# Holding result scatters back around the last norm, and giving each later product its own slot for one

## The chip, the cores and the metric

The kernel runs on one core of a Trainium2 chip. The time is device microseconds from start to end of one execution; of the kernel before there are six runs, median 702.27 us (700.46 to 706.06). Five engines work side by side, each with its own instruction queue in order: PE (TensorE, matrix products, with PEld for loading weights), DVE (VectorE), ACT (ScalarE), POOL (GpSimd) and SP (SyncE, which here only issues DMAs). They wait for each other through semaphores. DMAs move data between DRAM and the on-chip memory; indirect ones (scatter and gather by an index per row) are issued by POOL.

## The reference

The input x has 8 sequences of 512 tokens of width 128, in float32. Three residual blocks follow one another:

```
x = x + 0.5 * ffn(layernorm(x))
x = x + attention(layernorm(x))          # 16 heads of 8, causal, decay on half of the heads
x = x + 0.5 * ffn(layernorm(x))
```

The `ffn` is a mixture of 8 experts (128 -> 512 -> 128, relu) of which each token uses two: the router takes the two largest of eight logits and weighs the two results with a softmax over them:

```
logits = x @ router_w + router_b
topk_scores, topk_idx = top_k(logits, 2);  gates = softmax(topk_scores)
out = sum_e gate_e * (relu(x @ W1[e] + b1[e]) @ W2[e] + b2[e])
```

The reference computes all experts for all tokens; the kernel computes only the two that count.

## The kernel before

**Groups and rooms.** The tokens of the eight sequences are sorted to experts in groups: f0, f1, f2 for the first ffn, g0, g1, g2 for the second. Each expert has a room of fixed size in a DRAM buffer of the group (`xs`); for g1 and g2 it has 512 rows, in four tiles of 128. A group is filled by *token scatters* (`scatter` in `route`, L895): one indirect DMA for 128 tokens and one of their two experts, so 8 for a sequence. When all of a group's token scatters have landed, `experts` (L948 on) loads the rooms one expert at a time (`fetch`, L957), transposes them (`turn`, L1000, copied to `xT` at L1004), multiplies by W1 (`wide`, four products of 512 columns, L1013, relu at L1020) and by W2 (`out`, four tiles, L1037, bias added on DVE at L1041). Each of these is one *piece*; g1 and g2 have 72 pieces each, nine for a middle expert: four of the first product, four of the second product of the expert before, one of transposes.

**Results.** In g1 and g2 (the "tagged" groups) each row carries the number of its token's place. Each of the 32 tiles of results is sent back to that place in a second DRAM buffer (`ys`) by a *result scatter* (`send`, L981), an indirect DMA too. `out` only appends it to the list `results`. Later `collect` reads `ys` back in plain order (`yr`, L1140), multiplies by the gates, adds to x (L1144, L1148, L1154) and writes the output (L1157). The result tiles `ysb` have five buffers, one for each expert in flight.

**Order.** The order is written out by hand. The main part is a row of *units*: 96 units (0 to 95) are attention steps, units from 96 to 125 have no attention any more. `surround(n, att)` writes one unit: the attention step if there is one, a quota of pieces of the group that is being computed, the steps that are due in that unit (`due`: norm, router, projection, read-back, each a generator that is advanced by one step), and up to three *transfers*. `plan` says which group is opened in which unit (`close_group` and the first two `fetch`es), and between which units its pieces are spread: g1 from unit 79 to 106, g2 opened in unit 106 and spread from 107 to 125.

**Transfers.** `transfer` takes one indirect DMA from a list: token scatters and gathers (`jobs`) come first, results (`results`) when there are none. It is called at fixed places of a unit: after the first piece, in the middle (only from unit 96 on, when more than two wait), and at the end. POOL's queue takes them in the order in which they are written. `behind_mark` (L640 on) makes every one wait for the latest evacuation of a product that was written before it (`mark`), so a transfer can't start long before the place where it was written.

**The last sequence.** Sequence 7's attention is finished in unit 98. Its second norm and router (`route`) run three steps a unit: the norm in unit 99 (the reciprocal root of the variance, `rstd`, is a POOL instruction, L479, DVE's `xn` at L774 waits for it), transposes (L789), logits (L825) and ranks in unit 100, places (L869 to L885) in unit 101, where its eight token scatters join the list. They are the last of g2. Before, units 98 to 100 send eight results and unit 101 one before the first token scatter; the eight follow in units 101 to 103, each behind another piece; then results again, three a unit.

**The end.** After unit 125 the rest of the results is sent, then g2's read-back runs.

Of the kernel before, what the change touches and what calls it, by code (L numbers as in the profile page):

```python
# [49 lines left out]
CAP = max(cap for _, cap, _ in ROOMS)  # L50
NOWHERE = 1e6
CT = -(-CAP // P)
STOP = object()

def common_constants(nc, const, aps, names):
# [393 lines left out]
class Group:  # L449
# [3 lines left out]
    def __init__(self, shares, cap, key, xs, ys, tagged):  # L453
        self.shares, self.cap, self.key, self.xs, self.ys = shares, cap, key, xs, ys
        self.base, self.tiles = [], 0
        for _, t0, t1 in shares:
            self.base.append(self.tiles)
            self.tiles += t1 - t0
        self.tagged, self.width = tagged, D + 2 * tagged
        self.ct = -(-cap // P)  # L460
        self.rows = cap // self.ct
        assert self.ct * self.rows == cap
        self.parts = [(t, min(3 if cap > 4 * P else 4, self.ct - t))
                      for t in range(0, self.ct, 3 if cap > 4 * P else 4)]
        self.placed = 0
        self.pieces = E * (len(self.parts) * (1 + C) + self.ct) + 1


# [19 lines left out]
class Main:  # L488
    def __init__(self, tc, ctx, aps):
# [15 lines left out]


        self.jobs, self.results, self.mark = deque(), deque(), None
        self.adds, self.unit = deque(), 0
        const = self.const

# [144 lines left out]
    def transfer(self, second=False):  # L655

        if self.jobs and (
            not second or any(urgent for urgent, _ in self.jobs)
            or (len(self.jobs) > 4 and not self.results)
        ):  # L660
            self.jobs.popleft()[1]()
        elif self.results:
            self.results.popleft()()

    def additions(self):
# [282 lines left out]
    def experts(self, g):  # L948
# [31 lines left out]
        def send(e, t, ys):  # L980
            ins = nc.gpsimd.indirect_dma_start(  # L981
                out=g.ys[:, :],
                out_offset=bass.IndirectOffsetOnAxis(ap=home[e][:rows, t : t + 1], axis=0),
                in_=ys[:rows, t, :], in_offset=None,
            ).ins
            tc.declare_no_dep(ins, group=f"ys_{key}", reason="no two rows have the same home")
            tc.add_to_no_dep_group(f"ys_{key}", ins)
            self.in_turn(ins, scatter=True)
            self.behind_mark(ins)

        def up(e, xb):

# [3 lines left out]
            def turn(t0, nt):  # L996
                n0, n = t0 * rows, nt * rows
                tp = self.bank([P, N], f"xbT_ps_{key}_{e}_{t0}")
                for t in range(nt):
                    nc.tensor.transpose(  # L1000
                        tp[:, ts(t, rows)], xb[:rows, t0 + t, :D], self.ident[:rows, :rows]
                    )
                if self.evac == "act":
                    nc.scalar.copy(xT[:, n0 : n0 + n], tp[:, :n])  # L1004
                else:
                    nc.vector.tensor_copy(xT[:, n0 : n0 + n], tp[:, :n])
                if g.tagged and t0 == 0:
                    homes(e, xb)

            def wide(t0, nt, c):  # L1010
# [10 lines left out]
                else:  # L1021
                    ins = nc.vector.tensor_scalar(dst, z[:, :n], bias, 0.0, ALU.add, ALU.max)  # L1022
                self.mark = ins.ins

            return (
                h, [partial(turn, *p) for p in g.parts],
# [3 lines left out]
        def down(e, h):  # L1030
# [3 lines left out]
            def out(t):  # L1034
# [7 lines left out]
                    ys[:rows, t, :], y[:rows], self.b2_sb[:rows, e], ALU.add  # L1042
                )
                self.mark = ins.ins
                if g.tagged:
                    self.results.append(partial(send, e, t, ys))
                elif t == g.ct - 1:
                    nc.sync.dma_start(
                        g.ys[: E * g.cap, :].rearrange("(t p e) d -> e p t d", p=rows, e=E)[e],
                        ys[:rows, : g.ct],  # L1050
                    )
# [75 lines left out]
    def collect(self, g, i, dst, parts=1):  # L1127
# [5 lines left out]
        if i % 2 == 0:  # L1133
            self.pair = self.p2.tile([P, 2, T, 2, D], FP, tag="ee", name=f"yr_{b}")
        yr = self.pair[:, i % 2]
        src = g.ys[: 2 * P * g.tiles, :].rearrange("(t p r) d -> p t r d", p=P, r=2)
        n = -(-(end - first) // parts)
        for t in range(first, end, n):
# [202 lines left out]
def macaron_kernel(  # L1341
# [51 lines left out]
    with ExitStack() as main:  # L1393
# [61 lines left out]
        def combined(u, g, i, dst=None, urgent=False, ahead=False):  # L1455
# [2 lines left out]

        plan = [
            (f0, first, first, -16), (f1, -17, -16, 7), (f2, 5, 7, 43), (g0, 41, 43, 79),  # L1460
            (g1, 78, 79, tail - 1), (g2, tail - 2, tail - 1, ends),
        ]
        fills = {}

        def surround(n, att):

# [24 lines left out]
            m.evac = "dve" if att and n % seq not in (8, 9, 10) else "act"  # L1491
            if att:
                m.causal(units[n][2], ee, 0)
            run(take(fill, 1 if quota else 0))
            m.evac = "act"
            m.transfer()
            if last is not None:
                m.outputs(*last)
            if att:
# [5 lines left out]
            for k, (stream, steps) in enumerate(work):  # L1505
                some = todo // (len(work) - k + 1)
                run(take(stream, steps))
                run(take(fill, some))
                todo -= some
            if n >= core and len(m.jobs) + len(m.results) > 2:  # L1510
                run(take(fill, todo // 2))
                todo -= todo // 2
                m.transfer(second=True)
            run(take(fill, todo))
            m.additions()
            m.transfer(second=True)

        m.held = m.oT = None
        with m.banks(("m", 8)):
# [35 lines left out]
            for i in range(2):  # L1555
                combined(79 + 7 * i, g0, i, out)
            for i, (_, t0, t1) in enumerate(g1.shares):
                at(tail + 2 + 3 * i, m.collect(g1, i, out), 1 + t1 - t0)
            at(tail, m.verdict(bad), 2)

            for u in range(first, 0):
# [74 lines left out]
```

## Time and profile before

| | us |
|---|---|
| median of six runs | 702.27 (700.46 to 706.06) |
| profiled execution | 704.29 |
| its span, first to last instruction | 702.6 |
| PE busy in the span | 625.2 (89%) |
| POOL busy in the span | 295.6 (42%) |
| last product result evacuated on DVE | 683.2 |
| last result scatter landed | 688.06 |

The profile shows one execution. A line of its timeline gives the start and the length in us, the engine, the line of the kernel, the operation, what it writes `<-` what it reads, and in brackets how long the engine had stood idle and what ended that. A line of the waits gives who waited for whom, the total in us, how often, and the longest. A line of the stretches gives the stretch, its length, and for each engine the time it was busy in it with the number of instructions, then the clock granted to TensorE as a share of full speed, the share of time in which the DMA engines were busy, and GB/s. POOL counts an indirect DMA as busy for the time in which it issues it (about 0.97 us). TensorE's ends are modelled, not measured.

### The profile page before, as it was taken

To read this page: it belongs to the slowest core of one execution; us is meant where nothing else is said; L and a number is where in the kernel's file an instruction comes from. 1 tells how busy PE (TensorE), PEld (TensorE's weight loads), DVE (VectorE), ACT (ScalarE), POOL (GpSimd) and SP (SyncE) were. 2 spreads that over 40 slices of the span, in tenths; PEclk is the share of its full clock that TensorE was granted. 3 is DMA by queue.
4 is the path that set the end of the run, shared out by engine and by line. 5 is a ranking of instruction groups with operands and counts; after the bars stand their busy time and mean duration, and the time that the engine had idled before them with its cause. 6 is when DMAs were issued, how large, how long until landed. Compare 5 with 4: busy or idle time off the path is not lost. (4 is left out here: it accounts for less than half of the span.)

```text
span 702.6 us, 12913 instructions
## 1 busy us (share of the span) xinstructions
PE 625.2 (89%) x4797; PEld 406.0 (58%) x4797; DVE 411.5 (59%) x1426; ACT 347.7 (49%) x564; POOL 295.6 (42%) x318
## 2 busy tenths in 40 slices
PE   3269989999999999999989999999999988869980
PEld 2148857755656565556656656555565656647760
DVE  6736437745466575685677687778665644232433
ACT  4034333455565656556566565656746532234422
POOL 3744626654041214414143524332244455654550
PEclk9999999999999999999999999999999998979995
DMA  8746833221508961011201111112112021144225
GB/s 256 199 134 188 224 106 97 70 63 56 119 27 141 186 201 34 27 27 45 68 28 43 42 39 36 32 32 81 49 32 62 28 61 39 58 125 138 73 70 156
DMA packets 80230, 61.33 MB, mean 87 GB/s; under 512 B 7400, under 2 KB 73888, under 8 KB 80160
## 3 DMA queue, kind: packets, MB, share of 16 engines
q1 hardware_dynamic: 71296, 42.79, 23.8%
q0 software_dynamic: 8576, 17.63, 8.2%
q8 instruction: 40, 0.66, 0.4%
q14 instruction: 30, 0.25, 0.1%
q10 hardware_dynamic: 288, 0.01, 0.0%
HBM read 26.21 MB, written 34.19 MB: 86 GB/s over the span
## 5 line engine op out<-in xcount | busy, mean ns | idle before, releaser
L1245 ACT ACTIVATE ee<-st 128x768 f32<-128x768 f32 (+1 forms) x192 | 158.9, 880 | 93.2 <-PE st L1238 80.7
L1252 DVE TENSOR_TENSOR ee<-ee,keep 128x256 f32<-128x256 f32 (+1 forms) x192 | 97.9, 511 | 98.0 <-ACT ee L1245 92.7
L479 POOL DMA_INDIRECT yt_f<-ys,back_f x64 | 65.2, 1019 | 130.0 <-ACT h_f L1020 49.5
L1037 PEld LDWEIGHTS y_f<-w_sb,h_f 128*120 128x120 f32 (+1 forms) x704 | 85.9, 182 | 28.3 <-issue 15.8
L1238 PE MATMUL st<-qT,kT 32*128 32x512 f32 (+3 forms) x1024 | 96.1, 467 | 5.2 <-ACT ee L1245 3.2
L895 POOL DMA_INDIRECT xs<-xn_g,to_g x64 | 64.0, 1000 | 86.0 <-DVE x L1098 13.5
L1037 PEld LDWEIGHTS y_g<-w_sb,h_g 128*128 128x128 f32 x640 | 81.8, 194 | 31.1 <-issue 24.4
L1013 PE MATMUL z_g<-xT_g,w_sb 128*128 128x512 f32 (+1 forms) x192 | 90.3, 557 | 6.3 <-ACT xT_g L1004 6.3
L1037 PE MATMUL y_f<-w_sb,h_f 128*120 128x128 f32 (+1 forms) x704 | 94.0, 277 | 0.2 <-DVE h_f L1022 0.2
L1013 PE MATMUL z_f<-xT_f,w_sb 128*128 128x480 f32 (+1 forms) x192 | 91.3, 566 | 1.0 <-ACT xT_f L1004 1.0
L1264 PE MATMUL o<-ee,vpad 128*32 128x512 f32 (+3 forms) x1024 | 90.1, 444 | 1.1 <-DVE ee L1252 1.0
L1020 ACT ACTIVATE h_f<-z_f,b1T 128x480 f32<-128x480 f32 (+1 forms) x86 | 53.4, 622 | 68.0 <-PE z_f L1013 45.5
L1037 PE MATMUL y_g<-w_sb,h_g 128*128 128x128 f32 x640 | 86.5, 280 | 0.2 <-DVE h_g L1022 0.2
L981 POOL DMA_INDIRECT ys<-ysb_g,home_g x64 | 62.8, 981 | 51.1 <-ACT h_g L1020 20.4
L1020 ACT ACTIVATE h_g<-z_g,b1T 128x512 f32<-128x512 f32 (+1 forms) x77 | 49.3, 642 | 52.7 <-PE z_g L1013 42.6
L1238 PEld LDWEIGHTS st<-qT,kT 32*128 32x128 f32 x1024 | 43.1, 183 | 38.0 <-issue 15.4
L1041 DVE TENSOR_TENSOR ysb_g<-y_g,b_sb 128x128 f32<-128x128 f32 x80 | 23.0, 290 | 70.9 <-PE y_g L1037 47.5
L895 POOL DMA_INDIRECT xs<-xn_n,to_f x40 | 39.1, 977 | 37.9 <-issue 8.8
L1264 PEld LDWEIGHTS o<-ee,vpad 128*32 128x32 f32 x1024 | 23.9, 109 | 53.1 <-issue 15.1
L1041 DVE TENSOR_TENSOR ysb_f<-y_f,b_sb 120x128 f32<-120x128 f32 (+1 forms) x88 | 25.1, 289 | 49.8 <-PE y_f L1037 38.0
L1013 PEld LDWEIGHTS z_g<-xT_g,w_sb 128*128 128x128 f32 x192 | 30.4, 196 | 26.0 <-issue 15.5
L1013 PEld LDWEIGHTS z_f<-xT_f,w_sb 128*128 128x128 f32 x192 | 31.4, 200 | 15.4 <-issue 11.0
(187 smaller groups left out, 773.2 us busy)
## 6 DMA issues: line engine op xcount, KB each, us to landing
xs<-zeros SPq DMA_DIRECT2D x8, 520.0 KB
xb_g<-xs SPq DMA_DIRECT2D x16, 260.0 KB
w_sb<-in_L_ffn_W_dram SPq DMA_DIRECT2D x16, 256.0 KB
xb_f<-xs SPq DMA_DIRECT2D x16, 240.0 KB
ys<-ysb_f SPq DMA_DIRECT2D x16, 240.0 KB
ys<-zeros SPq DMA_DIRECT2D x2, 1664.0 KB
x<-in_L_attn_x_dram SPq DMA_DIRECT2D x8, 256.0 KB
xs<-zeros SPq DMA_DIRECT2D x1, 1920.0 KB
```

Of the source, the lines that this page charges most:

```text
L479: ins = op(*args, **kw)
L895: ins = nc.gpsimd.indirect_dma_start(out=g.xs[:, :], out_offset=bass.IndirectOffsetOnAxis(ap=to[:, t, r : r + 1], axis=0), in_=xn[:, t, : ...
L981: ins = nc.gpsimd.indirect_dma_start(out=g.ys[:, :], out_offset=bass.IndirectOffsetOnAxis(ap=home[e][:rows, t : t + 1], axis=0), in_=ys[:r ...
L1013: nc.tensor.matmul(z[:, :n], self.w1_sb[:, e, ts(c, P)], xT[:, n0 : n0 + n], start=True, stop=True,)
L1020: ins = nc.scalar.activation(dst, z[:, :n], AF.Relu, bias=bias)
L1037: nc.tensor.matmul(y[:rows], h[:, c, ts(t, rows)], self.w2_sb[:, e, c, :], start=(c == 0), stop=(c == C - 1),)
L1041: ins = nc.vector.tensor_tensor(ys[:rows, t, :], y[:rows], self.b2_sb[:rows, e], ALU.add)
L1238: nc.tensor.matmul(st[:, h, c0 : c0 + N - kt * P], kT[r0 : r0 + SLOT, ts(kt, P)], qT[r0 : r0 + SLOT, kt * P :], start=True, stop=True,)
L1245: nc.scalar.activation(ee[:, two, :width], st[:, two, :width], AF.Exp)
L1252: ins = self.nc.vector.tensor_tensor(d, d, self.keep.unsqueeze(1).unsqueeze(1).to_broadcast([P, 2, len(parts), P]), ALU.min,)
L1264: self.nc.tensor.matmul(self.o[h * SLOT : (h + 1) * SLOT, kt * P :], self.vpads[b % 2][:, kt, 4 * g + h, :], ee[:, h, c0 : c0 + n], start= ...
```

## The change

It has five parts, all behind or near the end of the 96 attention units.

1. `HOLD`: in units 97, 98 and 99 no result is sent (token scatters still are).
2. From unit 100 on the fixed places for transfers are gone. The token scatters that are in the list after a step are written at once, all in a row.
3. From unit 100 on a new wrapper, `pieces`, may send one result after each piece: when the counter `work` is at least `SPACING` (830), it calls `transfer` and takes 830 off. `work` counts the columns (or for transposes and results the like) of every piece written.
4. g2 is opened (count, and the first two loads) in unit 105, not 106. Its pieces still begin in unit 107.
5. g1's four read-backs begin in units 113, 116, 119 and 122, not 110, 113, 116 and 119. An assertion says that all results of the group have been sent by then.

```diff
--- before.py
+++ after.py
@@ -50,6 +50,8 @@
 CAP = max(cap for _, cap, _ in ROOMS)
 NOWHERE = 1e6
 CT = -(-CAP // P)
+SPACING = 830
+HOLD = (97, 98, 99)
 STOP = object()
 
 def common_constants(nc, const, aps, names):
@@ -462,7 +464,7 @@
         assert self.ct * self.rows == cap
         self.parts = [(t, min(3 if cap > 4 * P else 4, self.ct - t))
                       for t in range(0, self.ct, 3 if cap > 4 * P else 4)]
-        self.placed = 0
+        self.placed = self.sent = 0
         self.pieces = E * (len(self.parts) * (1 + C) + self.ct) + 1
 
 
@@ -505,6 +507,7 @@
 
 
         self.jobs, self.results, self.mark = deque(), deque(), None
+        self.work = 0
         self.adds, self.unit = deque(), 0
         const = self.const
 
@@ -659,7 +662,7 @@
             or (len(self.jobs) > 4 and not self.results)
         ):
             self.jobs.popleft()[1]()
-        elif self.results:
+        elif self.results and self.unit not in HOLD:
             self.results.popleft()()
 
     def additions(self):
@@ -987,6 +990,7 @@
             tc.add_to_no_dep_group(f"ys_{key}", ins)
             self.in_turn(ins, scatter=True)
             self.behind_mark(ins)
+            g.sent += 1
 
         def up(e, xb):
 
@@ -1004,6 +1008,7 @@
                     nc.scalar.copy(xT[:, n0 : n0 + n], tp[:, :n])
                 else:
                     nc.vector.tensor_copy(xT[:, n0 : n0 + n], tp[:, :n])
+                self.work += nt * rows
                 if g.tagged and t0 == 0:
                     homes(e, xb)
 
@@ -1021,6 +1026,7 @@
                 else:
                     ins = nc.vector.tensor_scalar(dst, z[:, :n], bias, 0.0, ALU.add, ALU.max)
                 self.mark = ins.ins
+                self.work += n
 
             return (
                 h, [partial(turn, *p) for p in g.parts],
@@ -1042,6 +1048,7 @@
                     ys[:rows, t, :], y[:rows], self.b2_sb[:rows, e], ALU.add
                 )
                 self.mark = ins.ins
+                self.work += C * D
                 if g.tagged:
                     self.results.append(partial(send, e, t, ys))
                 elif t == g.ct - 1:
@@ -1133,6 +1140,7 @@
         if i % 2 == 0:
             self.pair = self.p2.tile([P, 2, T, 2, D], FP, tag="ee", name=f"yr_{b}")
         yr = self.pair[:, i % 2]
+        assert g.sent == E * g.ct
         src = g.ys[: 2 * P * g.tiles, :].rearrange("(t p r) d -> p t r d", p=P, r=2)
         n = -(-(end - first) // parts)
         for t in range(first, end, n):
@@ -1458,9 +1466,17 @@
 
         plan = [
             (f0, first, first, -16), (f1, -17, -16, 7), (f2, 5, 7, 43), (g0, 41, 43, 79),
-            (g1, 78, 79, tail - 1), (g2, tail - 2, tail - 1, ends),
+            (g1, 78, 79, tail - 1), (g2, tail - 3, tail - 1, ends),
         ]
         fills = {}
+
+        def pieces(fill, n):
+
+            for _ in take(fill, n):
+                if m.unit > HOLD[-1] and m.work >= SPACING:
+                    m.transfer()
+                    m.work = max(m.work - SPACING, 0)
+                yield
 
         def surround(n, att):
 
@@ -1491,9 +1507,11 @@
             m.evac = "dve" if att and n % seq not in (8, 9, 10) else "act"
             if att:
                 m.causal(units[n][2], ee, 0)
-            run(take(fill, 1 if quota else 0))
+            run(pieces(fill, 1 if quota else 0))
             m.evac = "act"
-            m.transfer()
+            slots = n <= HOLD[-1]
+            if slots:
+                m.transfer()
             if last is not None:
                 m.outputs(*last)
             if att:
@@ -1505,15 +1523,18 @@
             for k, (stream, steps) in enumerate(work):
                 some = todo // (len(work) - k + 1)
                 run(take(stream, steps))
-                run(take(fill, some))
+                while m.jobs and not slots:
+                    m.transfer()
+                run(pieces(fill, some))
                 todo -= some
-            if n >= core and len(m.jobs) + len(m.results) > 2:
+            if slots and n >= core and len(m.jobs) + len(m.results) > 2:
                 run(take(fill, todo // 2))
                 todo -= todo // 2
                 m.transfer(second=True)
-            run(take(fill, todo))
+            run(pieces(fill, todo))
             m.additions()
-            m.transfer(second=True)
+            if slots:
+                m.transfer(second=True)
 
         m.held = m.oT = None
         with m.banks(("m", 8)):
@@ -1555,7 +1576,7 @@
             for i in range(2):
                 combined(79 + 7 * i, g0, i, out)
             for i, (_, t0, t1) in enumerate(g1.shares):
-                at(tail + 2 + 3 * i, m.collect(g1, i, out), 1 + t1 - t0)
+                at(tail + 5 + 3 * i, m.collect(g1, i, out), 1 + t1 - t0)
             at(tail, m.verdict(bad), 2)
 
             for u in range(first, 0):
```

## The prediction

> **What bounds the kernel now.** The page first:
>
> ```profile
> span 702.6 us, 12913 instructions
> PE 625.2 (89%) x4797; PEld 406.0 (58%) x4797; DVE 411.5 (59%) x1426; ACT 347.7 (49%) x564; POOL 295.6 (42%) x318
> ```
>
> TensorE is the bound nearly everywhere, so the question is where it stands still. The diff acts from unit 97 on (about 582 us), so I read busy time by stretches there, with the granted clock after POOL's column. I cut the stretches at 3.41 us, because the clock changes only at such borders:
>
> ```profile
> 587.29:590.71 3.42, 1.47 (x7) 0.66 (x5) 1.73 (x7) 0.13 (x1) 2.84 (x4) 1.00 0.10 32
> 590.71:594.12 3.41, 2.88 (x13) 2.88 (x14) 1.41 (x4) 0.02 (x1) 2.60 (x3) 0.50 0.13 44
> 594.12:597.53 3.41, 3.41 (x16) 2.31 (x15) 1.88 (x9) 1.25 (x2) 0.76 (x1) 0.50 0.08 24
> ...
> 611.19:614.60 3.41, 0.92 (x9) 0.72 (x7) 0.29 (x1) 0.00 (x0) 2.67 (x3) 1.00 0.41 110
> ...
> 618.01:621.43 3.42, 0.00 (x0) 0.00 (x0) 0.68 (x4) 0.56 (x1) 0.79 (x2) 0.50 0.17 54
> ...
> 624.84:682.87 58.03, 57.99 (x344) 42.89 (x342) 20.35 (x79) 25.04 (x38) 30.32 (x32) 1.00 0.31 94
> ```
>
> The first number after the length is TensorE. There are two holes, near 588 and 611 to 622, each followed by half clock; from 624.8 to 682.9 it is full. Next the POOL queue's order in time:
>
> ```profile
> 586.73 0.97 POOL L981 DMA_INDIRECT ys<-ysb_g,home_g  x1 [0.31 <-issue]
> 587.72 1.04 POOL L479 TENSOR_TENSOR rstd_g<-var_g,neg_half 128x4 f32<-128x4 f32 x1
> 588.97 1.08 POOL L981 DMA_INDIRECT ys<-ysb_g,home_g  x1 [0.20 <-issue]
> ...
> 598.08 0.99 POOL L981 DMA_INDIRECT ys<-ysb_g,home_g  x1 [0.35 <-DVE posb_g L871]
> 600.09 0.97 POOL L895 DMA_INDIRECT xs<-xn_g,to_g  x1 [1.01 <-DVE ex_g L931]
> ```
>
> The last norm's `rstd` stands behind result scatters (L981). DVE had `var_g` at 585.67 and goes on only at 588.80 (row `xn_g`, "3.13 <-POOL rstd_g"). The eight last token scatters (L895) start at 600.09 and the eighth at 610.04. Behind them waits the first load of group g2. The waits from 584 to 625 us say so, and show one more thing:
>
> ```profile
> ACT xT_g L1004 <- remote: 12.8, 1, 12.8
> ...
> PE z_g L1013 <- ACT xT_g L1004: 4.9, 1, 4.9
> ...
> PE xbT_ps_g L1000 <- DMA xb_g<-xs: 3.4, 1, 3.4
> DVE xn_g L774 <- POOL rstd_g L479: 3.1, 1, 3.1
> ```
>
> g2's first transposes start at 615.49, when the load lands; they end at 616.58 by the model, yet ACT copies them only at 620.87 and the product starts at 621.51. These 4.3 us ("remote": a semaphore event with no instruction to name) have no cause in the trace. It happens while four 260 KB loads (issued 612.40 to 614.21) and an unbroken row of POOL scatters are in flight.
>
> ```profile
> 685.72 2.33 DMA ys<-ysb_g,home_g
> 688.07 0.34 SPq L1140
> 688.47 2.78 DMA yr<-ys
> ```
>
> The chain's end: the last result scatter releases g2's read-back; what follows (14.5 us) isn't touched.
>
> **The change, part by part.** I counted the written order unit by unit. *No results in units 97 to 99.* Before, nine result scatters stand between token scatters of sequences 6 and 7 (584.19 to 598.08); afterwards four (three in unit 100, one in 101). POOL is then idle from 582.2, `rstd` starts at 585.7 instead of 587.72, and `xn_g` moves from 588.80 to 586.78: 2.0 us earlier. TensorE's transposes then start when its product ends (587.58), not at 589.21: its 1.6 us hole closes. The 0.8 us for the copy of `xnT` stays.
>
> *The clock.* The stretch from 587.29 had 43% busy and was followed by half clock; the stretch 577.05 to 580.46 had 2.03 of 3.41 us (60%) and was not. Moved 2.0 us forward, the router's products fall into the stretch and make it about 2.65 of 3.42 us (77%): I take full clock, since 60% was enough. At half clock the router's products took 1.88 us, up to DVE's read at 593.15; at full about 1.0 (estimate: halved). Then the logits are read at 590.2, the mask is ready at 592.8 (same 2.6 us of DVE), the positions at 593.5, the tags at 594.5 (1.04 us after, as before): 4.2 us earlier. If half clock comes anyway, it is only 2.35 earlier; that is the near end.
>
> *The eight token scatters in a row.* POOL's fourth result scatter waits for the evacuation that ends at 593.5 and runs 593.75 to 594.7; after the usual 0.30 the tokens start at 595.0. The row 603.68 to 610.04 shows the pitch without waits: 1.27. The eighth starts at 595.0 + 7 x 1.27 = 603.9 against 610.04: 6.1 us earlier (near end 4.4). Nothing between them waits; queued behind them on POOL are 16 result scatters of g1, until 595.0 + 24 x 1.27 = 625.5. Who waits for those: the result buffers (five; g2's second expert writes at about 625 into what was sent by 611) and g1's read-back. Neither is late.
>
> *The load of g2 one unit earlier.* Two loads on SP (0.36 us each), the count matmul (0.17) and its DVE read (0.15) move past two g1 products. SP has nothing else there: it waited 45.9 us for the scatters, so the issue still follows the last landing. Cost and gain nothing by itself. The load lands as long after as before, so the transposes can start at 615.49 - 6.1 = 609.4. TensorE ends g1 at 612.1 - 1.6 - 2.7 (half clock ended) = 607.8, so the load still ends last, with 1.6 us of waiting instead of 3.4. Term: **-6.1**, bounds -4.4 and -6.1.
>
> *The late transposes.* Bounds: as long as before (0) or gone (-4.3, and with them the half clock around, -2.0: transposes 1.09 against 0.60, product 2.08 against 1.02, transposes 1.06 against 0.60). The nearest row is before's own place: after the change the same four loads again run beside POOL scatters at the same pitch. I take 0.
>
> The page "TensorE: Matmul & The Clock Gate" of the Trainium skill (Part 1: The HAM clock gate) has the clock fall only after an idle window of about 3.4 us. The row at 587.29 (43% busy, then half clock) contradicts it. By that rule the shorter wait before g2's transposes would keep full clock and add about -2.0; I go by the row, which leaves that loss as it is.
>
> *Results after each piece.* `work` grows from the start of the program and is never reset: up to unit 99 it is about 8 x (3,291 + 2 x 4,448 + 2,304) + 53 x 512 = 143,000. Each piece adds 512 and each call takes 830, so in 92 pieces it never falls below 830: the spacing never holds a result back. A result goes out behind its own product. In g2 TensorE is full anyway (57.99 of 58.03), and POOL needs 4 x 1.27 = 5.1 us of an expert's 7.4: hidden. At the end it counts: before, the last expert's scatters start at 681.90 to 685.72, behind one that waited its turn until 680.63. Now that one follows its evacuation (679.58) at 679.8, and the last starts at 679.8 + 4 x 1.27 = 684.9. Term: **-0.8**.
>
> *g1's read-back three units later.* Four loads (L1140), 26 multiply-adds (0.36 us) and four output DMAs move past twelve g2 products, on SP past the loads of experts 5 to 7 (which now no longer stand behind a read-back). The last pair of adds (0.73) lands between the last two evacuations on DVE: 681.97 + 0.29 + 0.73 = 682.99 against 682.90, +0.1. SP's 0.38 us issue of the output is covered by the 5 us to the last landing. If TensorE were not ahead there it would cost up to 0.7.
>
> Sum: -6.1 - 0.8 + 0.1 = -6.8. The profiled execution took 704.29 (span 702.6, 1.7 around it); that gives 697.5. It was 2.0 above the median of the six runs (702.27; 700.46 to 706.06), and the steps don't depend on that, so **695.5**.
>
> **Rivals.** *The clock stays half* (0.16): near ends above, -4.4 - 0.7 = -5.1: 697.2. Against it: 77% busy; for it: most of the stretch would be transposes and eight-column products, and the border's phase moves between executions.
>
> *The late results vanish* (0.19): if they hang on the coincidence, 6.1 us of shift may break it. -6.8 - 4.3 - 2.0 = -13.1: 689.2. For it: no other group's start shows "remote"; against: loads and scatters still meet.
>
> *Slower: POOL's unbroken row holds TensorE* (0.15). The late results fall into a row of twelve scatters at 1.27 us (604.96 to 618.67), and the copy comes 2.2 us after its end. Afterwards the row has 24 and ends at 625.5. If its end sets the copy, that is 627.7 instead of 620.87: +6.8 - 0.7 = +6.1: 708.4. It decides as soon as the copy comes after 621.6. Against it: the row of eight at 571 to 582 held nothing back, and scatters beside single loads after 640 don't either.
>
> *Nothing comes of it* (0.10): a cause between these two eats the gain at 606 to 622: within 3.5 us of 702.3.
>
> *It doesn't do what it says*: true of the spacing, by the count above, and priced in: a hold of one piece (0.9 us) would only undo the last term.
>
> **How the numbers follow.** Main case 0.40 at 695.5; its own range 693 to 697. 0.5% (3.5 us) is about what a measurement of this kernel tells from no change. Faster: 0.40 + 0.16 + 0.19 = 0.75; same 0.10; slower 0.15. The range takes in the three gains and half of the fourth: 688.5 to 701.0, leaving out 0.20.
>
> **What would show it.** `rstd` next to `var_g`, `xn_g` 2 us after it; full clock in the stretch behind; eight L895 at 1.27 us with no gap; "xb_g<-xs" landing about 6 us earlier; the last L981 less than 2.3 us after the last evacuation. Wrong, if token scatters wait (on POOL's order or an evacuation), if the "remote" wait of ACT grows, or if DVE begins to wait for result buffers.

## The result, and the profile after

The changed kernel takes 707.58 us (median of 20 runs, 702.89 to 711.19), the kernel before beside it 702.94 (46 runs): a ratio of 1.0062, 95% interval 1.0046 to 1.0078. It is slower by 0.6%, and the interval lies clear of 1; 695.5 was forecast. The profiled execution took 708.26 us. Its page begins:

```profile
span 706.6 us, 12909 instructions
PE 623.0 (88%) x4797; PEld 404.2 (57%) x4797; DVE 411.4 (58%) x1426; ACT 347.8 (49%) x564; POOL 295.7 (42%) x318
```

Busy time by stretches, the first two cut where the prediction cut them, the last at borders of the clock in this execution (after the stretch and its length: TensorE, its weight loads, DVE, ACT, POOL, the granted clock, DMA share, GB/s):

```profile
587.29:590.71 3.42, 2.64 (x20) 2.11 (x19) 2.21 (x8) 0.12 (x1) 1.71 (x2) 0.96 0.06 19
590.71:594.12 3.41, 3.41 (x17) 2.37 (x16) 2.39 (x9) 1.27 (x2) 0.85 (x2) 0.54 0.08 24
594.12:610.90 16.78, 11.96 (x73) 8.41 (x69) 3.76 (x20) 3.55 (x6) 12.82 (x14) 1.00 0.27 78
610.90:624.55 13.65, 3.41 (x16) 3.41 (x17) 0.74 (x3) 0.69 (x1) 7.91 (x9) 0.50 0.28 89
```

The 0.96 and 0.54 show that the clock fell about 0.3 us ahead of 590.71 here. The hole near 588 has shrunk from 1.95 us to 0.78. The other, around 611 to 622 before, is now a standstill from 608.3 to 621.1. The POOL queue in order of time (start, length, line, what it does, in brackets the idle time before it):

```profile
585.81 1.04 POOL L481 TENSOR_TENSOR rstd_g<-var_g,neg_half 128x4 f32<-128x4 f32 x1 [3.65 <-DVE var_g L771]
...
596.10 0.97 POOL L898 DMA_INDIRECT xs<-xn_g,to_g  x1 [0.30 <-issue]
...
605.01 0.97 POOL L898 DMA_INDIRECT xs<-xn_g,to_g  x1 [0.30 <-DMA xs<-xn_g,to_g]
...
616.46 0.97 POOL L984 DMA_INDIRECT ys<-ysb_g,home_g  x1 [0.31 <-issue]
620.24 0.97 POOL L984 DMA_INDIRECT ys<-ysb_g,home_g  x1 [2.81 <-DVE ysb_g L1047]
```

`rstd` stands next to `var_g`, and the eight token scatters go out without a gap; the eighth starts at 605.01 against 610.04. That much is what the change is about, and it came. But from 593.55 to 617.43 nineteen scatters now follow each other 1.27 us apart. The waits from 575 to 640 us say what that goes with:

```profile
PE y_g L1043 <- ACT h_g L1025: 15.1, 2, 12.9
...
DVE ysb_g L1047 <- remote: 13.6, 2, 12.4
ACT h_g L1025 <- remote: 12.7, 1, 12.7
```

TensorE waits 12.9 us for a relu; ACT and DVE have waited as long for "remote", an event with no instruction to name. TensorE's own queue:

```profile
602.05 1.05 PE L1043 MATMUL y_g<-w_sb,h_g 128*128 128x128 f32 x8
...
607.80 0.49 PE L1043 MATMUL y_g<-w_sb,h_g 128*128 128x128 f32 x2 [2.21 <-ACT h_g L1025]
621.14 4.80 PE L1043 MATMUL y_g<-w_sb,h_g 128*128 128x128 f32 x26 [12.85 <-ACT h_g L1025]
625.77 0.60 PE L1004 MATMUL xbT_ps_g<-ident,xb_g 128*128 128x128 f32 x4
627.05 1.12 PE L1018 MATMUL z_g<-xT_g,w_sb 128*128 128x512 f32 x2 [0.68 <-ACT xT_g L1008]
```

I call a result late by the time from the modelled end of its product to the start of the instruction that reads it, where the reading engine stood idle just before. Within the row, results are 1.07 us late at 600.7, 1.61 at 602.1, 5.67 at 607.0; behind it one is 16.6 late at 619.7, that of the product at 602.05:

```profile
619.67 0.29 DVE L1047 TENSOR_TENSOR ysb_g<-y_g,b_sb 128x128 f32<-128x128 f32 x1 [12.36 <-remote]
```

TensorE had meanwhile started later products, the last at 607.80, until it lacked the relu. This result is read 2.2 us after the row's end (617.43); in the kernel before the copy came 2.2 us after the end of its row (620.87 against 618.67). The row ended there because the next scatter had to wait for that evacuation (its 2.81 us above).

Group g2's first product comes at 627.05 against 621.51: 5.54 us later. From there to the last evacuation (686.78) it takes 59.73 instead of 61.39 us, since full clock returns before g2's first product and not behind it. The chain's end:

```profile
688.87 2.76 DMA ys<-ysb_g,home_g
...
693.54 4.87 DMA yr<-ys
```

The last scatter follows the last evacuation by 2.09 instead of 2.82 us; what comes behind takes 17.73 instead of 16.88. Sum: +5.54 - 1.66 - 0.73 + 0.85 = +4.0, the difference of the spans.

### The profile page after: what moved, and what is told of

It is laid out like the page before. It is cut to its first block, busy times and chain, and to the rows that moved or that the text cites. A ratio compares the mean times of both kernels' runs of the same rounds, so it can differ in the third digit from the quotient of the medians.

```text
span 706.6 us, 12909 instructions
## 1 busy us (share of the span) xinstructions
PE 623.0 (88%) x4797; PEld 404.2 (57%) x4797; DVE 411.4 (58%) x1426; ACT 347.8 (49%) x564; POOL 295.7 (42%) x318
## 5 line engine op out<-in xcount | busy, mean ns | idle before, releaser
L1043 PE MATMUL y_g<-w_sb,h_g 128*128 128x128 f32 x640 | 88.1, 284 | 15.3 <-ACT h_g L1025 15.1
L1018 PE MATMUL z_g<-xT_g,w_sb 128*128 128x512 f32 (+1 forms) x192 | 88.8, 549 | 2.0 <-ACT xT_g L1008 2.0
```

What stands on the lines that cost most here:

```text
L1018: nc.tensor.matmul(z[:, :n], self.w1_sb[:, e, ts(c, P)], xT[:, n0 : n0 + n], start=True, stop=True,)
L1043: nc.tensor.matmul(y[:rows], h[:, c, ts(t, rows)], self.w2_sb[:, e, c, :], start=(c == 0), stop=(c == C - 1),)
```

## The experiments

The first theory was ROW: an unbroken row of POOL's scatters holds back TensorE's results until 1 to 2 us after its end. Its rivals were LOADS (the four loads of g2 do it), CHANCE (a coincidence of that place), and later START, COUNT and BUSY POOL, as the expectations name them. "The kernel before there" is its median in the same set of runs on the same chip. "One run" stands where there is only the profiled execution, without an interval. The three rows_memset runs leave a part of the output unsent, so their times can't be compared.

| run | time, us | the kernel before there | ratio (95%) | results late by more than 2 us from 580 us on |
|---|---|---|---|---|
| hold_only | 682.88 | 687.81 | 0.9933 (0.9911 to 0.9955) | none |
| eight_only | 686.17 | 687.81 | 0.9972 (0.9956 to 0.9989) | none |
| rows_g2 | 698.16 | 687.81 | one run | none |
| rows_memset | 679.13 | 687.81 | one run | none |
| before_b | 700.24 | 704.36 | one run | up to 9.5 |
| after_b | 707.99 | 704.36 | 1.0055 (1.0029 to 1.0081) | up to 18.2 |
| hold_only_b | 701.48 | 704.36 | 0.9969 (0.9939 to 0.9999) | up to 7.4 |
| rows_g2_b | 717.37 | 704.36 | one run | up to 9.5, in g2 up to 4.95 |
| after_rows5 | 690.25 | 688.94 | 1.0033 (1.0016 to 1.0051) | none |
| after_even | 689.76 | 688.94 | one run | none |
| rows_memset_b | 680.79 | 688.94 | one run | none |
| after_c | 706.99 | 704.39 | 1.0042 (1.0011 to 1.0072) | up to 16.7 |
| after_rows5_b | 705.69 | 704.39 | 1.0040 (1.0011 to 1.0068) | up to 4.7 |
| after_even_b | 702.40 | 704.39 | one run | 2.6, once |
| rows_memset_c | 695.54 | 704.39 | one run | up to 9.3, in g2 none |
| even2 | 683.79 | 689.82 | 0.9914 (0.9884 to 0.9944) | none |
| even2_b | 685.78 | 688.96 | 0.9956 (0.9939 to 0.9973) | none |
| after_d | 682.61 | 688.96 | 0.9903 (0.9887 to 0.9920) | none |

**The parts alone, and rows of growing length.** hold_only has the first part of the change:

```diff
+HOLD = (97, 98, 99)
...
-        elif self.results:
+        elif self.results and self.unit not in HOLD:
             self.results.popleft()()
```

eight_only has the second:

```diff
                 run(take(stream, steps))
+                while n > 99 and m.jobs:
+                    m.transfer()
                 run(take(fill, some))
```

rows_g2 is the kernel before up to unit 108, and then sends g2's results in rows of set length, the rest at the end:

```diff
+ROWS = {110: 2, 113: 5, 117: 7, 122: 9}
...
-        elif self.results:
+        elif self.results and self.unit < 108:
             self.results.popleft()()
+
+    def in_a_row(self):
+
+        for _ in range(ROWS.get(self.unit, 0)):
+            self.results.popleft()()
...
             m.transfer()
+            m.in_a_row()
```

rows_memset has the same rows of fills of a scratch tile in place of the scatters, and never sends g2's results:

```diff
+    def in_a_row(self):
+
+        for _ in range(ROWS.get(self.unit, 0)):
+            self.results.clear()
+            ins = self.nc.gpsimd.memset(self.qpad.rearrange("p t h s -> p (t h s)")[:, :BLANK], 0.0)
+            self.in_turn(ins.ins)
+            self.behind_mark(ins.ins)
```

> Kernel before with the hold in units 97 to 99 alone. The token scatters start about 3 us earlier (596 to 597 for 600.1), and the five results held back come behind them. ROW: the row behind the token scatters gets longer by up to five, results are late from about 605 to the row's end, time +1 to +6 us against before (ratio 1.001 to 1.009). LOADS: g2's transposes come 2 to 4 us earlier and the delay stays at 4.3 us: -2 to -4 us (ratio 0.994 to 0.997).

> Kernel before with the eight token scatters written in a row alone (results still at the old places). The eighth starts at about 608 for 610.0, but nothing breaks the row from the results before to those behind: about 16 in place of 12. ROW: results late from about 604, no gain, -1 to +3 us (ratio 0.999 to 1.004). LOADS: -1.5 to -2.5 us (ratio 0.9965 to 0.998).

> Kernel before, but in g2 the result scatters are written in rows of 2, 5, 7 and 9 (units 110, 113, 117, 122), none between, the rest at the end. No group is loaded there with four loads at once, and TensorE is full in this stretch. Theory ROW (an unbroken row of indirect DMAs on POOL delays TensorE's results from about the sixth on, until 1 to 2 us after the row's end): evacuations on time in the rows of 2 and 5 (at most 1 us late), 2 us or more late at the end of the row of 7, 4 us or more in the row of 9, and TensorE stands still for it. Theory LOADS (the late results come from the four 260 KB loads of a group's start meeting scatters): no evacuation later than 0.5 us in any row.

> As the run with rows of 2, 5, 7 and 9, but each scatter of a row is replaced by a fill of 1,500 elements per partition on POOL (about 1.2 us, estimated from 0.20 us for 128), and g2's results are not sent at all, so that part of the output is left out. ROW, if any busy POOL does it: the same delays as with scatters, 2 us or more in the rows of 7 and 9. ROW, if it takes indirect DMAs: no evacuation later than 0.5 us. LOADS: none late either.

These four ran on one chip, and there nothing was late: not in hold_only's row of 28 scatters (583.9 to 619.2), nor in eight_only's of 24 or rows_g2's of 17, while before, on the first chip, a row of 12 had been followed by results up to 9.5 us late. The kernel before took 687.81 us there, not 702. ROW as I had put it fell: it had expected 1.001 to 1.009 of hold_only and 0.999 to 1.004 of eight_only. LOADS, whose ratios come near, had expected the 4.3 us of delay to stay, and there was none. A fourth theory, CHIP, took the place of ROW: there are chips on which rows hold results back (the kernel before takes 702 to 704 us) and chips on which they don't (688 to 690). Without late results both parts gain, by 4.9 and 1.6 us.

**The same again, for the other kind of chip.**

> The kernel before, unchanged, profiled on this chip. The kernel before took 687.8 us where the first four experiments ran, and no result of TensorE was late there in rows of up to 28 scatters; in the first profile (702.6 us span) results were late in rows of 12. Theory CHIP (whether a row of indirect DMAs on POOL holds TensorE's results back depends on the chip): either about 700 to 704 us with late results at 610 to 621, or 686 to 690 us with none, the two together. Theory CHANCE (the late results are an event of single executions): late results and time don't go together.

> The changed kernel, unchanged, on the same chip as the kernel before. CHIP: where the kernel before takes about 688 us, all steps of the prediction come and nothing holds TensorE: -7 to -10 us (ratio 0.985 to 0.990); where it takes about 702, +3 to +6 us as in the first result (1.004 to 1.009). CHANCE: a ratio of 1.004 to 1.009 on any chip.

> Kernel before with the hold in units 97 to 99 alone, again. CHIP: at about 688 us before, ratio 0.991 to 0.996 as measured there; at about 702 us, the longer row costs what the earlier start gains or more: 1.000 to 1.009. CHANCE: 0.991 to 0.996 on any chip.

> Kernel before with g2's result scatters in rows of 2, 5, 7 and 9, again. CHIP: where the kernel before takes about 688 us no evacuation is late in any row (as measured); where it takes about 702, evacuations are late by 2 us or more in the rows of 7 and 9, away from any load of four rooms. CHANCE: none late in the rows on any chip.

This chip was of the 704 kind. before_b and after_b repeat the first two profiles: a row of 12 with results up to 9.5 us late, and a row of 19 (594.1 to 618.0) with up to 18.2. hold_only_b, with rows of 12 and 13, has 7.4 and 6.2, and gains just 0.3%; CHIP had expected 1.000 to 1.009, so it misjudged how the longer rows weigh against the earlier start. The clean test is rows_g2_b: in g2, where TensorE is otherwise full and no four loads start together. POOL's rows of seven and nine there, first and last scatter of each:

```profile
658.17 0.96 POOL L987 DMA_INDIRECT ys<-ysb_g,home_g  x1 [7.08 <-ACT h_g L1026]
...
665.84 0.97 POOL L987 DMA_INDIRECT ys<-ysb_g,home_g  x1 [0.30 <-issue]
...
684.99 0.97 POOL L987 DMA_INDIRECT ys<-ysb_g,home_g  x1 [0.30 <-issue]
```

And DVE's evacuations that come late:

```profile
668.17 0.51 DVE L1047 TENSOR_TENSOR ysb_g<-y_g,b_sb 128x128 f32<-128x128 f32 x2 [3.28 <-PE xbT_ps_g L1006]
...
686.11 0.29 DVE L1047 TENSOR_TENSOR ysb_g<-y_g,b_sb 128x128 f32<-128x128 f32 x1 [2.57 <-remote]
```

At 668.17 a result 2.67 us late is read, 1.4 us after the row of seven has ended (666.81); in the row of nine (674.8 to 686.0) results are 2.4 to 4.95 us late, until 1.6 us after its end. Behind the rows of two and five none is by more than 0.7. LOADS and CHANCE fall: the row was put there by hand, and the results followed it.

**Scatters, or any work of POOL?** rows_memset ran on both kinds of chip.

> The kernel before; in g2 POOL fills 1,500 elements of a scratch tile in rows of two, five, seven and nine such instructions in place of the result scatters, and g2's results are left unsent, so a part of the output is left out. Where the kernel before takes about 702 us: INDIRECT (it is the row of indirect DMAs that holds back TensorE's results): no result late by more than 1 us in g2 in any of the four rows, while rows of seven and nine scatters there gave 2.7 and 2.4 to 4.9 us. BUSY POOL (any unbroken work of POOL does): 2 to 5 us late at the rows of seven and nine. In both the row of twelve scatters ahead of g2 still makes results late, 9 us at the most. Where the kernel before takes about 688 us: none late under either, no more told than by the run on record.

> The kernel before; in g2 POOL fills 1,500 elements of a scratch tile in rows of two, five, seven and nine such instructions in place of the result scatters, and g2's results are left unsent, so a part of the output is left out. Where the kernel before takes about 702 us: INDIRECT: no result late by more than 1 us in g2 in any of the four rows; BUSY POOL: 2 to 5 us late at the rows of seven and nine, as with scatters there. The row ahead of g2, of scatters still, makes results late under both. Where the kernel before takes about 688 us: none late under either.

rows_memset_c's fills of seven and nine in g2 (start, length of the whole row):

```profile
656.50 9.79 POOL L671 MEMSET qpad<- 128x1500 f32 x7 [6.16 <-ACT h_g L1030]
673.14 12.60 POOL L671 MEMSET qpad<- 128x1500 f32 x9 [6.85 <-ACT h_g L1030]
```

They are longer than the rows of scatters (9.8 and 12.6 us against 8.6 and 11.1), and no result in g2 is 0.1 us late, though loads and read-backs on SP's queue go on in g2; in the same execution the row of twelve scatters ahead of g2 makes results 9.3 us late. BUSY POOL falls: it takes the DMAs. Whether a row of plain scatters from another queue would do it too wasn't run.

**The row broken, in the changed kernel.** Holding scatters back in the written order behind the tokens leaves POOL idle only if they wait for later products. So both versions send two results in unit 100, none up to unit 106, and then in g2 five for each nine pieces: after_rows5 behind five pieces in a row, after_even behind about every second piece. This is after_rows5; after_even has `(m.beat - 2) * 5 % 9 < 5` in the place of `(m.beat - 2) % 9 < 5`.

```diff
-                if m.unit > HOLD[-1] and m.work >= SPACING:
-                    m.transfer()
-                    m.work = max(m.work - SPACING, 0)
+                if m.unit == HOLD[-1] + 1 and m.beat < 2:
+                    m.transfer()
+                    m.beat += 1
+                elif m.unit >= tail - 1:
+                    if (m.beat - 2) % 9 < 5:
+                        m.transfer()
+                    m.beat += 1
                 yield
...
-                at(tail + 5 + 3 * i, m.collect(g1, i, out), 1 + t1 - t0)
+                at(tail + 8 + 2 * i, m.collect(g1, i, out), 1 + t1 - t0)
```

> The changed kernel, with its result scatters written in another place: two in unit 100, none from there to unit 106, and from unit 107 on (the start of group g2) five behind five pieces of g2 and none behind the next four, so that POOL's scatters come as one row of eight (the token scatters, 595 to 605) and then as rows of five with about 1 us between them; what is left goes out at the end, and g1's read-back starts at unit 116. ROW (an unbroken row of more than six or so scatters on POOL holds back TensorE's results until 1 to 2 us after the row's end): where the kernel before takes about 702 us, no result is more than 2 us late between 595 and 680, g2's first transposes start by 611 and its first product by 612.5 (the changed kernel: 625.8 and 627.1), TensorE has no idle stretch of 12 us, and its last product ends at about 669 to 671. Ten scatters are left by then, 12.7 us, so the last starts at about 680 to 683 and the whole takes 696 to 701. START (the late results belong to the start of g2 itself or to the end of g1, whatever POOL does): results 10 to 18 us late as in the changed kernel, first product at about 627, and 715 or more. COUNT (what counts is how many scatters go out in some tens of us, broken or not): results 5 us late or more come back inside g2 between 615 and 650. Where the kernel before takes about 688 us no result is late with either kernel, and this run tells only its time, 683 to 692.

> As the run with rows of five, but the five scatters of each nine pieces of g2 stand behind every second piece: the same number in the same time, with 0.3 to 0.5 us between two of them instead of 1 us after five. ROW: where the kernel before takes about 702 us no result is more than 2 us late, as with rows of five, if a gap of 0.3 to 0.5 us breaks a row; if only a longer gap does, the results come 2 to 8 us late in g2 and the run with rows of five has none. COUNT: late results as with rows of five. Time within 3 us of that run where no result is late.

> Rows of five, as in the run on record, where the kernel before took 688.9 us, this one 690.3, and no result was late (its last product was evacuated at 657, ten scatters were left and the last started at 669.6). Where the kernel before takes about 702 us: ROW expects no result more than 2 us late between 595 and 675, g2's first product by 612.5, no idle stretch of TensorE near 12 us, its last product at about 669 to 671, and 12 to 14 us behind that for the ten scatters left: 698 to 705 in all. START expects results 10 to 18 us late, the first product at about 627, and 715 or more. COUNT expects results 5 us late or more inside g2.

> The same five scatters of each nine pieces, evenly spaced (0.3 to 0.5 us between two). Where the kernel before takes about 702 us: ROW with any gap enough: no result over 2 us late; ROW with only a longer gap enough: 2 to 8 us late in g2, and none with rows of five; COUNT: late with both. Where it takes about 688 us: none late, within 2 us of the run with rows of five.

The first two ran on a chip of the 689 kind and tell only their times. The second two ran on one of the 704 kind. POOL and TensorE in after_even_b:

```profile
603.72 0.96 POOL L898 DMA_INDIRECT xs<-xn_g,to_g  x1 [0.30 <-issue]
609.38 0.96 POOL L984 DMA_INDIRECT ys<-ysb_g,home_g  x1 [4.70 <-DVE second_g L970]
```

```profile
609.17 0.63 PE L1004 MATMUL xbT_ps_g<-ident,xb_g 128*128 128x128 f32 x4 [0.40 <-DVE ysb_g L1047]
610.48 1.12 PE L1018 MATMUL z_g<-xT_g,w_sb 128*128 128x512 f32 x2 [0.68 <-ACT xT_g L1008]
```

With the row ended at 604.7, TensorE's waits ahead of g2 are 0.67 and 0.40 us, and g2's first product starts at 610.48: on the same chip after_c, with its row of 19, stands still for 11.86 us and has it at 625.56. Fifteen microseconds of TensorE's time ahead of g2 came back by moving scatters on POOL alone; START falls. In after_rows5_b the first product comes at 608.24, but in g2 its scatters fall behind their evacuations, the gaps close, and there are rows of six to nine with results 3.4, 2.3, 4.7 and 4.5 us late, against my bound of 2; after_even_b, with the same number in the same time and no row above five in g2 before 669, has 0.93 at the most there: in the written order evenly spaced, on POOL they come in rows of up to five with gaps of 0.6 to 1.3 us between rows. That is for ROW against COUNT. Ahead of g2 the row of eight token scatters still makes results up to 2.6 us late in after_even_b and 2.1 in after_rows5_b, a little over the bound. The totals gain little, since ten to twelve scatters are left when the products end: after_even_b's last one starts at 683.50. after_rows5_b took 705.69 us where ROW had expected 698 to 705.

**Fewer left over.** even2 keeps the even spacing, sends two more results in unit 99 and two in unit 106, and seven for each twelve pieces of g2:

```diff
-HOLD = (97, 98, 99)
+HOLD = (97, 98)
...
-            slots = n <= HOLD[-1]
-            if slots:
+            slots = n < 100
+            if n < 99:
                 m.transfer()
...
-                if m.unit == HOLD[-1] + 1 and m.beat < 2:
+                if m.unit == 100 and m.beat < 2 or m.unit == tail - 2:
...
-                    if (m.beat - 2) * 5 % 9 < 5:
+                    if m.beat * 7 % 12 < 7:
```

> The evenly spaced version with fewer scatters left for the end: four result scatters behind the norm's row and ahead of the tokens (two of them in unit 99) instead of two, two more in unit 106, and seven for each twelve pieces of g2 instead of five for each nine. Leftover at the end, by count: 12 less 2 less 2 less 1 or 2, so six or seven, and 6 x 1.27 = 7 us less behind the last product. Where the kernel before takes about 702 us: ROW, with the leftover as the only other cost, expects no result over 3 us late, g2's first product at 609 to 612, and 702.4 - 6 to 7 = 694 to 697 us, a ratio of 0.985 to 0.993. If the denser spacing makes rows again (COUNT), results are 3 to 8 us late in g2 and it takes 699 or more. Where the kernel before takes about 688 us: 689.8 - 6 to 7 = 682 to 685, a ratio of 0.989 to 0.996.

> As the run on record, which took 683.8 us where the kernel before took 689.8 (0.991). Where the kernel before takes about 702 us: ROW, with the scatters left over as the only other cost, expects no result over 3 us late, g2's first product at 609 to 612, and 694 to 697 us, a ratio of 0.985 to 0.993, with the changed kernel at 1.004 to 1.008 beside it. If the denser spacing makes rows again (COUNT), results are 3 to 8 us late in g2 and it takes 699 or more. Where the kernel before takes about 688 us: 0.988 to 0.995 again.

Both ran on chips of the 689 kind, at 0.9914 and 0.9956; the first is inside what was expected, the second just outside (0.995). On a chip of the 704 kind it wasn't tried, so that it beats both kernels there isn't shown. Of the versions that ran on both kinds only hold_only gains on both, on the 704 kind by 0.3% with an interval that ends at 0.9999. eight_only wasn't run there.

**The change itself on both kinds.**

> The changed kernel unchanged. Where the kernel before takes about 702 us: a ratio of 1.004 to 1.008, a row of 19 scatters and results up to 16 to 18 us late, as in the two runs there. Where it takes about 688 us: CHIP (the change is good in itself and loses by late results alone, which are not there) expects no result late, g2's first product 5 us or more before that of the kernel before, and 678 to 683 us, a ratio of 0.985 to 0.992. If the ratio is 1.00 or more there too, the loss isn't only that of late results, and ROW would be half an answer.

> The changed kernel unchanged. Where the kernel before takes about 688 us, no result is late in any row so far; CHIP expects none here, g2's first product 5 us or more before that of the kernel before, and 678 to 684 us, a ratio of 0.985 to 0.993. A ratio of 1.00 or more there would mean that late results aren't the whole of the loss. Where it takes about 702 us: 1.004 to 1.008 once more, with a row of 19 and results 16 to 18 us late.

after_c on the 704 kind is the third loss there (1.0042). after_d on the 689 kind gains: 0.9903. POOL in after_d, the first token scatter and the first result behind the eight:

```profile
584.96 0.97 POOL L898 DMA_INDIRECT xs<-xn_g,to_g  x1 [0.30 <-DVE ex_g L928]
...
595.14 0.97 POOL L984 DMA_INDIRECT ys<-ysb_g,home_g  x1 [0.30 <-DMA xs<-xn_g,to_g]
```

and TensorE:

```profile
599.42 0.95 PE L1004 MATMUL xbT_ps_g<-ident,xb_g 128*128 128x128 f32 x4 [1.95 <-DMA xb_g<-xs]
601.04 2.07 PE L1018 MATMUL z_g<-xT_g,w_sb 128*128 128x512 f32 x2 [0.68 <-ACT xT_g L1008]
```

The row has 35 scatters there (582.4 to 626.7), and no result is late. g2's first transposes wait 1.95 us for the load (1.6 was forecast), and the copy follows them at once. In rows_memset_b, which is the kernel before up to unit 108, the first product came at 605.32 on another chip of this kind, 4.28 us later. Counted from the start of attention's last exponential (557.32 and 555.42) it is 6.2 us; against rows_g2 and rows_memset, the same order on a third chip, it is 4.6 and 4.2. So the 5 us that were expected aren't shown, but a gain of 4 to 6 is.

## Why the prediction was wrong

**Right, step by step.** *No results in units 97 to 99*: `rstd` at 585.81 (585.7 forecast), `xn_g` at 586.89 (586.78), the router's products at 589.17 (589.2). *Eight token scatters in a row*: pitch 1.27 us; the first at 596.10 (595.0), the eighth 5.0 us earlier than before, between the bounds of 4.4 and 6.1. *The load one unit earlier*: its issue still follows the scatters, at 607.36 against 612.40. *Results after each piece*: the end behind the last evacuation is 0.73 us shorter (0.8), and the spacing holds nothing back. *g1's read-back later*: the last evacuations stay 0.89 us apart and the adds lie between them. *What comes behind the last scatter* isn't quite untouched, as I had put it: it took 17.5 to 17.8 us in four profiles of the changed kernel against 16.9 and 17.1 in two of the kernel before (17.8 in eight_only). Why is open.

**The clock.** I took full clock behind the stretch from 587.29, since TensorE would be busy in 2.65 of its 3.42 us. It was busy in 2.64, and half clock came all the same (0.54 in the next stretch). So 60% was enough at 577 and 77% was not at 587: the busy share doesn't decide it alone. It cost 1.1 us at the token scatters, inside the bounds.

The page "TensorE: Matmul & The Clock Gate" of the Trainium skill (Part 1: The HAM clock gate), by which the clock falls after an idle window of about 3.4 us, would have kept it full too; the row speaks against it a second time.

**The step that failed: "The late transposes".** I set it at 0 with bounds from -4.3 to 0, on the ground that the same four loads would again run beside scatters. The bounds lacked the other sign. The row grew from 12 scatters to 19, the lateness from 9.5 to 16.7 us, and the forecast gain of 6.1 turned into a loss of 5.5. The rival "POOL's unbroken row holds TensorE" had the right cause, and a sum near the result (708.4 against 707.58, or +6.1 against +4.6) by a way that was only partly so: I let the row run to 625.5 with the copy at 627.7. It ended at 617.43, but the late relu left 5 us of g1's products to do, and g2's first product came at 627.05.

I gave that rival 0.15 and argued that "the row of eight at 571 to 582 held nothing back". The profile of before says otherwise:

```profile
578.10 0.29 DVE L1041 TENSOR_TENSOR ysb_g<-y_g,b_sb 128x128 f32<-128x128 f32 x1 [2.25 <-PE xbT_ps_g L1000]
...
610.11 0.29 DVE L1041 TENSOR_TENSOR ysb_g<-y_g,b_sb 128x128 f32<-128x128 f32 x1 [1.54 <-PE cnt_ps_g L945]
```

The row at 571 is five unbroken scatters (571.0 to 577.2), and a result 1.11 us late is read at 578.10, 0.9 us behind its end. In the row of twelve, evacuations were 0.97 us late at 610.11 and 3.66 at 613.7; the first lies ahead of the first load's issue at 612.40, which already told against the loads. I had looked at the "remote" wait alone, the last and longest of a series that grew with the row.

**What the other chips add.** Where no row holds results back, the change gives what I had added up: -6.4 us (0.9903) against -6.8. hold_only and eight_only give -4.9 and -1.6 there, -6.5 together. So the sum was right but for that one term, and that term exists on one kind of chip only. How near the totals come is in part luck: what comes behind the last scatter, which stood in no term, varies from 16.5 to 17.8 us among these profiles.

## What to carry to other kernels

When a change closes the gaps in a queue of indirect DMAs, list what else in the profile happens inside and just behind such rows, and give the cost bounds of both signs: here results were 1 to 2 us late behind a row of five, up to 9.5 in one of twelve, and 16 to 18 in one of nineteen. A wait without a named releaser is best read as a series over the whole profile, by how late each result is read, and not at its largest member. A gain below 1% is to be measured on more than one chip: the same change gave 1.004 to 1.006 on some and 0.990 on another.

## What the runs showed of the hardware

The chips were of two kinds for this program. On four the kernel before took 687.8 to 689.8 us, and no row of scatters, of up to 35, delayed a result from 580 us on; on two, and in the first comparison, it took 702.9 to 704.4, and rows of six to nine delayed results by 1.5 to 5 us, longer ones by up to 18. In the ten profiles on the first kind no idle engine reads one of the experts' products or transposes more than 0.14 us after its end; in the ten on the other kind six to 22 of the 247 to 270 such reads of products come more than 1 us after theirs. As far as the record names the chips, none was used in two sets of runs; whether this is a property of the chip or of its state at that time isn't shown. Of the 15 us between the kinds some 10 are there by the end of the attention's last exponential (563.5 to 569.2 us against 555.4 to 558.3); late results behind rows of five and six scatters (2.2 us at 88.5, 1.5 at 119.4) are among what the profiles show up to there, but I didn't account for all of it.

What holds the results back in the chip stays open. POOL goes on meanwhile, and so does DVE with work that needs no product: in after_rows5_b it adds at 652.45 while a product that ended at 651.07 is read only at 655.79. Fills on POOL don't do it, and the trace has no instruction or transfer for the time between a product's end and the event that lets its reader go. That the products themselves ended later than the model puts them isn't excluded by the trace either, though in the profile after TensorE started later products at 603.99 and 607.80 while the one of 602.05 was read at 619.67.
